# Zeros and scales of the down weights in one table row, two transfers a granule

## The chip, the cores and the metric

The kernel runs on one core of a Trainium2 chip. The metric is the device time of one execution in microseconds (us). Five engines work side by side, each through its own instruction queue: TensorE (PE, with its weight loads PEld), VectorE (DVE), ScalarE (ACT), GpSimd (POOL) and SyncE (SP). Here SP computes nothing; it issues nearly all DMA transfers.

## What is computed

The input x has 2048 rows of 1024 numbers. Both branches start from the layer norm of x, and their sum is added to x:

```python
xn = _layernorm(x)
out = x + s4_conv(xn) + ffn(xn)

def dequantize(W_q, scale, zero):      # W_q: two 4-bit numbers a byte
    w = stack([W_q >> 4 & 15, W_q & 15], -1)
    w = w.reshape(out, -1, 64)         # groups of 64
    return (w - zero[:, :, None]) * scale[:, :, None]

def ffn(x):                            # hidden 1024, inter 2752
    g = x @ dequantize(gate).T
    u = x @ dequantize(up).T
    return (silu(g) * u) @ dequantize(down).T
```

`s4_conv` is a long convolution whose kernel of 1024 taps is itself computed from a small state-space model, plus a multiple of xn. What matters here are the down weights: 1024 x 2752 numbers of 4 bits, with one zero and one scale for every 64 of them.

## The kernel before

**Precision.** PE works in fp16. Activations and weights are split into a high and a low fp16 part, and each product is made of three matmul passes (high·high, high·low, low·high). Matrix products are cut in blocks of two by two and formed with seven products in place of eight, so operands are also needed as sums and differences of blocks.

**Stages.** Until about 160 us x is loaded, normalised, and the first tiles are worked. From there to about 876 us runs the *gate/up stage*: `NJ = 21` tiles of the inner dimension (index j), each for two halves of the rows (index cp), so a step is called j_cp, such as 18_1. Beside it, in the same stage, the down weights are prepared and the convolution's kernel is computed in small DVE operations (tiles `s4p`, `s4n`). From 888 to 1004 us PE does the convolution (`cv`), from 1004 to 1325 us the down products.

**A gate/up step** (`gate_up`, seven products, each of twelve matmuls of 128x512) uses four PSUM banks, named A, B, C, D with the step's number. The scheme is a chain: ACT copies A to B, C to hb and B to D in turn; product 5 finishes D, then DVE adds D to hb (`hb_18_1<-D18_1,hb_18_1`); product 4 finishes C, ACT copies it to ha, DVE adds B (`ha<-B,ha`) and multiplies by silu of A (`ha<-ha,A`); product 3 refills D. A bank can be filled again only when DVE or ACT has read it, so PE waits for hb or ha when these are late. Products 5, 4 and 3 of one step are issued among the products of the next step.

**Gate and up weights** come in granules (tiles `w2` to `w42`): a granule is unpacked by DVE, multiplied by its scales on ACT in sixteen small instructions (`w<-w,sz`), summed on DVE, cast to a high part (ACT, `nat`), subtracted for the low part (DVE, `nat<-w,nat`), and transposed by DMA (`wf<-nat`).

**Down weights** are `2 * NPAIR = 20` granules, w43 to w62, worked in ten pairs (ga, gb) such as (w52, w62) by the generator `load_wd`. From j = `WD_FROM = 4` on, four of its steps are taken in each j_cp. For every granule:

- `load` fetches packed numbers (`raw`).
- `fetch_wd` allots the tile `w` ([128, 8, 256] fp32; two such buffers exist) and loads zeros into the part `w[:, 0:4]` and scales into `w[:, 4:8]`. Both come out of the table `SZT` in DRAM and are spread by DMA over 64 partitions each: partitions 0 to 63 take one half of the table's row (b = 0), 64 to 127 the other (b = 1). Then DVE unpacks nibbles (`qn`), and a DMA transposes them (`raw<-qn`).
- `dequant` makes `x4 = q - zeros` (`w<-raw,w`, the *subtract*), then `x4 * scales` (`w<-w` on 128x1024, the *multiply*).
- After that come sums and differences, casts on ACT (`nd<-w`), low parts on DVE (`nd<-w,nd`), and stores `WD<-nd`.

Of a pair, ga is fetched near the end of the pair before, gb at the pair's own start.

**The table** is made once by `scales_t`: zeros and scales of all twenty granules are loaded (`t0`), DVE writes them in another order to `t1` (scales times 1024), transposes 32x32 blocks, and four transfers store the table. Its shape is `SZT [2*NPAIR, 2, 2, 8, 128]`, with axes granule, w (scale or zero), b, c, h.

**Order.** Instructions are not issued in the order of the source. The kernel is built under a tile framework with `schedule_with_timeline_sim=True`: a planner with its own model of each instruction's duration chooses the order on each engine's queue when the program is built, within data dependencies and buffer counts. On the chip each queue runs strictly in that order: an instruction that waits holds up everything behind it on its engine. Nearly every instruction is recorded through the helper class `Engine` and so appears as line L77.

Of the kernel before, what the change touches and what calls it, by code (L numbers as in the profile page):

```python
# [41 lines left out]
G_WD = G_MIX + 1  # L42
# [45 lines left out]
def build(nc, tc, x, xp, raw_d, sz_d, par_d, vct_d, tab_d, csrow_d, out):  # L88
# [3 lines left out]
    with es:  # L92
# [11 lines left out]
        SZT = dr.tile([2 * NPAIR, 2, 2, 8, P], F32, name="SZT")  # L104
# [10 lines left out]
        SP, G, PE = Engine(tc, nc.sync), nc.gpsimd, Engine(tc, nc.tensor)  # L115
# [22 lines left out]
        def wtemp(kind, shape, dtype, name):  # L138
            return home[kind].tile(shape, dtype, tag=kind, name=name, **({"bufs": szbufs[0]} if kind == "sz" else {}))
# [148 lines left out]
        with ea:  # L288
# [47 lines left out]
            def sums(w, b_side):  # L336

                op = ALU.subtract if b_side else ALU.add
                V.tensor_tensor(w[:, 4], w[:, 0], w[:, 2], ALU.subtract)
                V.tensor_tensor(w[:, 2], w[:, 2], w[:, 3], op)  # L340
                if b_side:
                    V.tensor_tensor(w[:, 5], w[:, 0], w[:, 2], ALU.subtract)
                else:
                    V.tensor_tensor(w[:, 5], w[:, 2], w[:, 0], ALU.subtract)
                V.tensor_tensor(w[:, 6], w[:, 1], w[:, 5], ALU.subtract)
# [91 lines left out]
            def scales_t():  # L437

                n = 2 * NPAIR
                t0, t1 = (wtemp("nat", [P, n, 2, 16], F32, f"szt{i}") for i in range(2))  # L440
                SP.dma_start(t0, sz_d[G_WD : G_WD + n].rearrange("n p w c -> p n w c"))

                for i in range(2):
                    src, dst = t0[:, :, i].rearrange("p n (c b) -> p n c b", b=2), t1[:, :, i].rearrange("p n (b c) -> p n c b", b=2)
                    V.tensor_scalar(dst, src, (WS, 1.0)[i], None, ALU.mult)
                V.transpose(t0.rearrange("p n w c -> p (n w c)"), t1.rearrange("p n w c -> p (n w c)"))
                for a in range(4):
                    SP.dma_start(
                        SZT.rearrange("n w b c h -> (w b c) n h")[:, :, 32 * a : 32 * a + 32],
                        t0[32 * a : 32 * a + 32].rearrange("p n w c -> p n (w c)"),  # L450
                    )

            def lag(n=1):

                n += len(tails)
                while len(tails) < n:
                    yield
# [3 lines left out]
            def load_wd(u):  # L461


                pr, kq = divmod(u, 2)
                ga, gb = (G_WD + 2 * p + kq for p in (pr, pr + NPAIR // 2))
                tt, sub = V.tensor_tensor, ALU.subtract

                def load(gi):
                    raw = rawd[gi] = wtemp("raw", [P, 16, 32], I32, f"raw{gi}")
                    SP.dma_start(raw, raw_d[gi].rearrange("p (a b) -> p a b", a=16))  # L470

                def fetch_wd(gi):


                    raw = rawd.pop(gi)
                    w = wtemp("wd", [P, 8, 256], F32, f"w{gi}")
                    for i in range(2):
                        for b in range(2):
                            SP.dma_start(w[64 * b : 64 * b + 64, 4 * i : 4 * i + 4].rearrange("p f c -> p (f c)"),
                                         SZT[gi - G_WD, 1 - i, b].rearrange("c h -> (c h)").partition_broadcast(64))  # L480
                    q = wtemp("raw", [P, 16, 2, 32], I16, f"qn{gi}")
                    low = raw.bitcast(I16).rearrange("p a (b c) -> p a b c", c=2)[:, :, :, 0]
                    V.tensor_scalar(q[:, :, 0, :], low, 4, 15, ALU.logical_shift_right, ALU.bitwise_and)
                    V.tensor_scalar(q[:, :, 1, :], low, 15, None, ALU.bitwise_and)
                    qt = raw.bitcast(I16).rearrange("p a b -> p (a b)").rearrange("p (a b) -> p a b", a=8)
                    SP.dma_start_transpose(qt, q.rearrange("p a b c -> p (a b c)"))
                    return w, qt

                def dequant(w, qt):
                    x4 = w[:, 0:4]  # L490
                    tt(x4, qt.rearrange("p (f a) b -> p f (a b)", f=4), x4, sub)
                    tt(x4, x4, w[:, 4:8], ALU.mult)

                blocks = lambda w: w.rearrange("p f (m c) -> p f m c", m=2)
                nats = {}

                def hi(i, src):
                    nats[i] = wtemp("nat", [P, 7, 2, P], F16, f"nd{u}_{i}")
                    A.copy(nats[i][:, :, 0], src)

                def lo(i, src):
                    nat = nats.pop(i)
                    tt(nat[:, :, 1], src, nat[:, :, 0], sub)
                    SP.dma_start(
                        WD2[i - 1][:, :, pr, kq].rearrange("f p a c -> p f (a c)"), nat.rearrange("p f a c -> p f (a c)")
                    )

                nxt = [G_WD + 2 * ((u + 1) // 2 + o) + (u + 1) % 2 for o in (0, NPAIR // 2)] if u + 1 < NPAIR else None
                if u == 0:
                    load(ga)  # L510
                    load(gb)
                    yield from lag()
                    ready_wd[ga] = fetch_wd(ga)
                    yield
                ready_wd[gb] = fetch_wd(gb)
                yield from lag(2 if u == 0 else 1)
                ma = ready_wd.pop(ga)
                with tc.issue_after(tails[-1].ins):
                    dequant(*ma)
                wa = blocks(ma[0][:, 0:7])  # L520
                yield
                sums(ma[0], True)
                hi(1, wa[:, :, 0])
                yield
                if nxt:
                    load(nxt[0])
                lo(1, wa[:, :, 0])
                tt(wa[:, :, 0], wa[:, :, 1], wa[:, :, 0], sub)
                hi(5, wa[:, :, 0])
                yield  # L530
                lo(5, wa[:, :, 0])
                mb = ready_wd.pop(gb)
                dequant(*mb)
                wb = blocks(mb[0][:, 0:7])
                yield
                sums(mb[0], True)
                hi(3, wb[:, :, 1])
                tt(wa[:, :, 1], wb[:, :, 1], wa[:, :, 1], sub)
                yield
                if nxt:  # L540
                    load(nxt[1])
                lo(3, wb[:, :, 1])
                hi(7, wa[:, :, 1])
                tt(wb[:, :, 1], wb[:, :, 1], wa[:, :, 0], sub)
                yield

                lo(7, wa[:, :, 1])
                hi(6, wb[:, :, 1])
                if nxt:
                    ready_wd[nxt[0]] = fetch_wd(nxt[0])  # L550
                yield
                hi(2, wb[:, :, 0])
                lo(6, wb[:, :, 1])
                yield
                lo(2, wb[:, :, 0])
                tt(wb[:, :, 0], wb[:, :, 0], wb[:, :, 1], sub)
                hi(4, wb[:, :, 0])
                yield
                lo(4, wb[:, :, 0])
                yield  # L560
# [406 lines left out]
            t0 = combine(0)  # L967
# [12 lines left out]
            run(combine(1))  # L980
            finish_h(1, 1, h1b, h1c)
            scales_t()
            early.close()
            we.close()
# [105 lines left out]
        for b in range(2):  # L1090
            for n in range(2):
                p0 = 64 * b + 32 * n
                base = KP[:, 128 - 64 * b - 62 - n :]
                src = bass.AP(base.tensor, base.offset, [[2, 32], [base.ap[0][0], 2], [1, 1024]])
# [15 lines left out]
        for a0, b0 in ((128, 384), (640, 384)):  # L1110
            a, b = ([band[:, i, c : c + 384] for i in range(2)] for c in (a0, b0))
# [67 lines left out]
        for cp in range(2):  # L1179
# [7 lines left out]
            for c in range(2):  # L1187
                for k in range(2):
                    a, b = ([xc[2 * c][:, i, m, :] for i in range(2)] for m in (k, k + 2))
# [219 lines left out]
```

## Time and profile before

| | us |
|---|---|
| median of three runs | 1329.95 |
| lowest and highest | 1327.34, 1331.86 |
| the profiled execution | 1331.74 |
| its span (first to last instruction) | 1330.0 |
| PE busy | 1274.0 (96%) |
| DVE busy | 987.9 (74%) |
| ACT busy | 669.2 (50%) |
| POOL busy | 182.8 (14%) |

The mean clock granted to PE is 0.990 of full speed. The share of busy time is an average over stages; what a change inside the gate/up stage is worth is read from PE's holes in that stage.

Some durations of single instructions that the argument uses are, from the timeline:

| engine | instruction | us |
|---|---|---|
| PE | twelve matmuls of one product, 128x512 | 2.75 |
| ACT | sixteen scalings `w<-w,sz` | 5.41 |
| ACT | a cast of 128x896 | 0.94 |
| DVE | subtract or multiply of a granule, 128x1024 | 1.22 |
| DVE | one operation on hb or ha, 128x512 | 0.68 |
| DVE | a low part, 128x896 | 1.09 |
| SP | issue of one `w<-SZT` (median) | 0.607 |

A line of the timeline gives start, duration, engine, source line, operation, output and inputs by the program's names, shape, and a count where several of a kind follow each other. In brackets stands how long the engine sat idle before it, and what released it. `SPq` is SP's queue of DMA issues; the duration there is that of the issuing, not of the transfer. How long a transfer takes from issue to landing is in the page's list of DMA issues.

### The profile page before, as it was taken

What the parts mean: (1) busy time and instruction counts of PE and PEld (TensorE: products, weight loads), DVE (VectorE), ACT (ScalarE), POOL (GpSimd) and SP (SyncE); (2) the same over time, 40 slices, a digit from 0 to 9 for tenths busy, and PEclk for the clock granted to TensorE, in tenths of its full rate; (3) what the DMA queues carried; (4) which work ended last, traced back from release to release, by engine and by line L of the source; (5) the groups of instructions that cost most, each with busy time, mean ns of one, the idle gap of its engine ahead of it and who ended that gap; (6) DMA issues with size and microseconds to landing.
All of it is one profiled execution on the core that took longest, in us unless ns stands there. A gap on an engine that the chain in (4) does not pass through costs nothing. (4 is left out here: it accounts for less than half of the span.)

```text
span 1330.0 us, 20904 instructions
## 1 busy us (share of the span) xinstructions
PE 1274.0 (96%) x7880; PEld 751.9 (57%) x7880; DVE 987.9 (74%) x1344; ACT 669.2 (50%) x1208; POOL 182.8 (14%) x267
## 2 busy tenths in 40 slices
PE   5999899999999899989989998999999999999998
PEld 5644344444444344444444443456558888888887
DVE  6779967486886877786878777462738898779792
ACT  4867566656656474766568475420204433443330
POOL 3230001010100000000111000000000032256440
PEclk8999899999999999999999998999999999999999
DMA  6791958469887988888798887765837779799981
GB/s 225 173 218 31 196 152 186 97 163 251 212 229 159 240 217 207 223 210 232 191 264 224 216 215 180 216 213 187 333 122 292 273 202 265 238 262 274 285 181 48
DMA packets 358401, 276.04 MB, mean 208 GB/s; under 512 B 211668, under 2 KB 304668, under 8 KB 354204
## 3 DMA queue, kind: packets, MB, share of 16 engines
q1 hardware_dynamic: 335676, 261.59, 70.6%
q0 software_dynamic: 21760, 10.49, 6.6%
q10 hardware_dynamic: 864, 2.62, 0.5%
q8 instruction: 62, 1.02, 0.3%
q14 instruction: 39, 0.32, 0.1%
HBM read 132.36 MB, written 94.84 MB: 171 GB/s over the span
## 5 line engine op out<-in xcount | busy, mean ns | idle before, releaser
L77 PEld LDWEIGHTS <-wf 128*128 128x128 f16 x3960 | 375.7, 99 | 467.8 <-issue 45.2
L77 PEld LDWEIGHTS <-g 128*128 128x128 f16 x2940 | 287.6, 98 | 33.5 <-issue 0.2
L77 ACT ACTIVATE w<-w,sz 128x64 f32<-128x64 int32 x640 | 217.9, 427 | 74.9 <-DVE w L77 58.3
L77 PE MATMUL A<-x,wf 128*128 128x512 f16 x912 | 215.2, 385 | 13.4 <-ACT ha L77 5.3
L77 PE MATMUL D<-x,wf 128*128 128x512 f16 x912 | 211.5, 380 | 14.1 <-DVE hb L77 12.1
L77 PE MATMUL C<-x,wf 128*128 128x512 f16 x912 | 208.0, 381 | 2.8 <-DVE ha L77 2.6
L77 ACT CAST g<-a 128x2560 f16<-128x2560 f32 x42 | 97.5, 2324 | 182.1 <-PE cv L77 52.6
L77 PE MATMUL A<-b,g 128*128 128x256 f16 x1680 | 185.9, 273 | 0.0
L77 DVE TENSOR_TENSOR w<-w 128x256 f32<-128x256 f32 (+2 forms) x272 | 136.9, 527 | 61.2 <-ACT w L77 54.7
L77 DVE TENSOR_TENSOR g<-a,g 128x2560 f16<-128x2560 f32 x42 | 118.4, 2821 | 30.9 <-ACT g L77 30.9
L1261 POOL DMA_DIRECT2D out<-o x64 | 78.8, 2139 | 360.7 <-DVE o L77 348.2
L322 POOL TENSOR_SCALAR sz<-sz 128x16 f32<-128x16 f32 x42 | 18.6, 443 | 673.2 <-DMA sz<-in_sz 622.7
L77 PE MATMUL B<-x,wf 128*128 128x512 f16 x456 | 106.7, 384 | 1.8 <-ACT B L77 1.8
L77 ACT CAST nat<-w 128x896 f16<-128x896 f32 x76 | 68.3, 935 | 72.9 <-issue 34.4
L77 ACT CAST nd<-w 128x896 f16<-128x896 f32 x70 | 64.1, 933 | 68.9 <-DVE w L77 47.6
L77 DVE TENSOR_TENSOR nat<-w,nat 128x896 f16<-128x896 f32 x76 | 81.0, 1087 | 19.3 <-ACT nat L77 19.1
L77 PE MATMUL D<-b,g 128*128 128x256 f16 x840 | 94.0, 273 | 0.0
L77 DVE TENSOR_TENSOR nd<-w,nd 128x896 f16<-128x896 f32 x70 | 75.5, 1086 | 16.3 <-ACT nd L77 16.0
L77 PEld LDWEIGHTS <-x 128*128 128x128 f16 x576 | 52.4, 98 | 23.7 <-issue 2.7
L77 DVE SCALAR_TENSOR_TENSOR p<-cv,p 128x512 f32<-128x512 f32 x32 | 21.9, 688 | 50.3 <-PE cv L77 44.9
L77 PE MATMUL cv<-band,x 128*128 128x512 f16 (+3 forms) x384 | 57.1, 299 | 0.0
L77 PE MATMUL g<-x,wf 128*128 128x128 f16 (+1 forms) x336 | 48.8, 293 | 1.7 <-ACT wf L82 0.8
(145 smaller groups left out, 1203.8 us busy)
## 6 DMA issues: line engine op xcount, KB each, us to landing
a<-HF SPq DMA_DIRECT2D x28, 1280.0 KB, 8.1
WD<-nd SPq DMA_DIRECT2D x70, 448.0 KB, 4.4
b<-WD SPq DMA_DIRECT2D x49, 640.0 KB, 5.9
w<-SZT SPq DMA_DIRECT2D x80, 256.0 KB, 5.7
raw<-in_raw SPq DMA_DIRECT2D x65, 256.0 KB, 3.8
HF<-ha SPq DMA_DIRECT2D x54, 256.0 KB, 2.9
HF<-s SPq DMA_DIRECT2D x40, 256.0 KB, 3.0
HF<-hb SPq DMA_DIRECT2D x36, 256.0 KB, 3.6
```

What stands on the lines that cost most here:

```text
L77: return method(*args, **kw)
L322: G.tensor_scalar(sz[:, 0], sz[:, 0], WS, None, ALU.mult)
L1261: G.dma_start(dst, o[:, q], accum_op=ALU.add)
```

## The change

The axes of the table become granule, b, i, c, h, where i = 0 is the zeros and i = 1 the scales. For one granule and one b, zeros and scales now lie side by side in 8 KB, as they do in the tile `w`. `fetch_wd` loads a granule with two transfers (64 partitions times 8 KB, 512 KB each) instead of four (64 partitions times 4 KB, 256 KB each). `scales_t` writes `t1` in the matching order.

```diff
-    for i in range(2):
-        src, dst = t0[:, :, i].rearrange("p n (c b) -> p n c b", b=2), t1[:, :, i].rearrange("p n (b c) -> p n c b", b=2)
+    t2 = t1.rearrange("p n w c -> p n (w c)").rearrange("p n (b i c) -> p n i c b", b=2, i=2)
+    for i in range(2):
+        src, dst = t0[:, :, i].rearrange("p n (c b) -> p n c b", b=2), t2[:, :, 1 - i]
         V.tensor_scalar(dst, src, (WS, 1.0)[i], None, ALU.mult)
...
     for a in range(4):
         SP.dma_start(
-            SZT.rearrange("n w b c h -> (w b c) n h")[:, :, 32 * a : 32 * a + 32],
+            SZT.rearrange("n b i c h -> (b i c) n h")[:, :, 32 * a : 32 * a + 32],
             t0[32 * a : 32 * a + 32].rearrange("p n w c -> p n (w c)"),
         )
...
-    for i in range(2):
-        for b in range(2):
-            SP.dma_start(w[64 * b : 64 * b + 64, 4 * i : 4 * i + 4].rearrange("p f c -> p (f c)"),
-                         SZT[gi - G_WD, 1 - i, b].rearrange("c h -> (c h)").partition_broadcast(64))
+    for b in range(2):
+        SP.dma_start(w[64 * b : 64 * b + 64].rearrange("p f c -> p (f c)"),
+                     SZT[gi - G_WD, b].rearrange("i c h -> (i c h)").partition_broadcast(64))
```

## The prediction

> **What bounds the kernel now.** I read the busy tenths of the page first, then the windows by stage, then who waits for whom, then the timeline round the longest waits.
>
> ```profile
> PE   5999899999999899989989998999999999999998
> DVE  6779967486886877786878777462738898779792
> PEclk8999899999999999999999998999999999999999
> ```
>
> Each digit is 33 us. TensorE (PE) is full almost throughout, and after about 876 us nothing else matters: the down products there have a busy PE from end to end. The windows (start:end, length, busy us of PE, PEld, DVE, ACT, POOL, then clock, DMA share, GB/s) say the same:
>
> ```profile
> 400.00:500.00 100.00, 91.91 (x443) 42.12 (x442) 77.14 (x126) 63.08 (x136) 7.89 (x18) 1.00 0.82 205
> 600.00:700.00 100.00, 92.84 (x422) 41.09 (x421) 76.62 (x128) 62.04 (x133) 9.54 (x15) 0.98 0.90 230
> 760.00:830.00 70.00, 63.52 (x282) 28.10 (x281) 51.14 (x78) 46.86 (x104) 3.17 (x9) 0.95 0.81 206
> 1004.00:1325.00 321.00, 321.00 (x2940) 287.49 (x2939) 254.58 (x169) 117.77 (x63) 98.41 (x80) 1.00 0.84 238
> ```
>
> So only PE's holes between 160 and 876 us can be won, some 6 to 8% of a window. What makes them, and what the table has to do with them, is in the waits (total us, times, longest) and in the table's row (shortest/median/longest issue in ns):
>
> ```profile
> PE D L77 <- DVE hb L77: 12.1, 4, 5.5
> DVE w L77 <- DMA w<-SZT: 32.9, 10, 8.3
> L77 SPq DMA_DIRECT2D w<-SZT x80: 445/607/2390, 165.8 to 799.3; - x80
> w<-SZT SPq DMA_DIRECT2D x80, 256.0 KB, 5.7
> ```
>
> VectorE (DVE) idles 32.9 us for the table, but an idle DVE costs nothing unless PE needs what is queued behind. The timeline shows where it does (start, length, what, idle before and its releaser):
>
> ```profile
> 796.76 3.17 SPq L77 DMA_DIRECT2D w<-SZT  x4
> 803.71 1.23 DVE L77 TENSOR_TENSOR w<-raw,w 128x1024 f32<-128x1024 int16 x1 [8.28 <-DMA w<-SZT]
> 804.86 0.68 DVE L77 TENSOR_TENSOR hb<-D,hb 128x512 f32<-128x512 f32 x1
> 805.59 1.86 PE L77 MATMUL D<-x,wf 128*128 128x512 f16 x4 [5.46 <-DVE hb L77]
> ```
>
> Granule w62: four transfers issued from 796.76, its subtract waits 8.28 us for zeros, hb_18_1 stands behind that subtract, and PE waits 5.46 us for the PSUM bank that hb_18_1 frees. Two smaller cases have the same shape, w56 and w60:
>
> ```profile
> 453.37 2.75 PE L77 MATMUL D<-x,wf 128*128 128x512 f16 x12 [2.58 <-DVE hb L77]
> 690.01 2.32 PE L77 MATMUL D<-x,wf 128*128 128x512 f16 x10 [3.41 <-DVE hb L77]
> ```
>
> **The change, part by part.** *Building the table* (scales_t, once, near 160 us): the same two scalings, one transpose and four writes; only destination strides differ. Priced 0: the nearest rows, these instructions themselves, are 0.45 us each, so the bounds are ±0.5. PE is covered by j = 2 and 3 there.
>
> *Loading it* (20 granules). Bytes stay at 1 MB a granule. Removed are 40 issues on SP's queue at 0.607 us, 24 us in all, 1.2 us a granule. SP is not on the chain except where a transfer is late, so this shows only through landing times. In the trace a granule's issues are 0.5 to 1.3 us apart and its four landings about 1.1 us apart (w60: the last three at 685.0, 686.2, 687.2).
>
> Here the Trainium skill speaks on both sides ("DMA: Bandwidth & Descriptors"). Section "Rules for kernel authors" says to coalesce many small transfers; section "Anatomy of one DMA" gives each a fixed cost of about 2 us. Two fewer would then bring 4 us a granule. The row says no: four 256 KB transfers land 1.1 us apart, so that cost overlaps, and the engines are full in these bursts (DMA share 1.13 in 340 to 350 us). The same section says that a completion is reported only after the last byte, which speaks **against** the change. Today zeros land some 2.2 us ahead of the granule's last transfer, and the subtract starts on them. Afterwards it needs both whole transfers. By the coalescing rule the subtract starts 1.8 us earlier (4 less 2.2), by the rows 1.0 later (2.2 less the 1.2 of saved issues). I take the rows. Packets grow from 4 to 8 KB; no SZT row shows that, so it is bounded: nothing gained, or 1.3 us a granule (8 KB packets of other transfers took 351 ns on average where two 4 KB SZT packets take 2 × 255; 128 packets on 16 engines). I take 0, since the landings are spaced as the bytes are.
>
> So the multiply, which always needed everything, may start about 1.2 us earlier, and the subtract 1.0 later. Alone this is a small loss on DVE.
>
> *Order.* What decides is that instruction order is chosen by a planner when the program is built, and it knows the new waits. Comparing both programs engine by engine: same instructions apart from the 40 issues, but from j = 6 on (after about 328 us) many stand in another order on DVE, ACT and PE. I walk through the places where PE stalls or where the order changes what PE needs, adding durations of the rows (subtract and multiply 1.22, hb or ha operation 0.68, twelve matmuls 2.75, sixteen ACT scalings 5.41). Ends are in brackets.
>
> - **w54, 329 to 339 us.** hb_6_1 now precedes the waiting subtract; ha_6_1, behind it, comes 0.5 earlier. PE's 1.32 stall at 339.0 shrinks: −0.5 (−1.6 to +0.3).
> - **w56, 446 to 463 us.** Now a reciprocal (1.75) and an ha operation fill the wait and hb_9_1 directly follows the subtract, no longer a multiply and a qn unpack (1.98 together). The 2.58 stall becomes about 1.5; ha_9_1 (1.81 stall at 463.1) also comes earlier. −1.9 (−3 to −0.5).
> - **j = 12/13, w58, 545 to 580 us.** Against the change: ACT now does w27's sixteen scalings before the ha_11_1 copy, and w28's fifteen and two nd casts before the hb_12_1 copy, while PE moves ten C12_1 matmuls ahead of A13_0. A new stall of some 3.3 us near 555, of which the old 2.0 at 559.9 is part, and 0.3 at w58: +1.5 (0 to +4).
> - **619 us.** C14_0 covers with five matmuls instead of nine while PE waits for ha_13_1 (3.02 now): four at 0.22 = +0.9 (0 to +2).
> - **w60, 675 to 698 us.** The fetch moves up about 3 us, and D15_1 is moved behind twenty-four matmuls of j = 16, 5.2 us of cover for the 3.41 stall. Late next: ha_15_0, behind w60's subtract, multiply and unpack. −2.5 (−3.4 to 0).
> - **w61, 732 to 755 us.** On SP the fetch is moved behind a weight transpose, an HF and a WD store; the fourth transfer, issued 14 us after the first (746.47), vanishes. Both w61 operations now precede hb_17_0, which PE needs only at 749.6 though it was done at 740.7. 0 (cover 9 us).
> - **w62, 785 to 820 us.** hb_18_1 and w52's subtract precede w62's, so PE's bank is free near 801. Late next: ha_18_1, behind w62's subtract and about four sums and multiplies. The whole granule lands near 804.5, so ha_18_1 ends near 811.9, and A19_1 starts there, not at 816.09: −4.1 (−7 to 0).
>
> Clock: "TensorE: Matmul & The Clock Gate", section "Part 1", has the clock halve after an idle window of about 3.4 us. The rows are less orderly:
>
> ```profile
> 340.00:350.00 10.00, 10.00 (x41) 4.18 (x39) 9.62 (x16) 10.00 (x24) 0.75 (x1) 0.83 1.13 222
> 690.00:700.00 10.00, 9.99 (x47) 4.57 (x47) 9.97 (x19) 3.02 (x5) 2.61 (x3) 1.00 0.92 229
> 800.00:810.00 10.00, 4.54 (x12) 1.61 (x11) 6.29 (x9) 1.84 (x5) 1.58 (x4) 0.72 0.54 131
> ```
>
> The third figure from the right is the granted clock: 0.72 after the 5.46 stall, 0.83 after one of only 1.32, 1.00 after 3.41. By the rule the 3.1 us that I leave before A19_1 keeps full clock, and −4.1 stands; by the rows a shorter stall can halve it, for up to 3.4 us of lost work, and −0.7 is left. I take −4.1, since w62's loss today followed the longest stall.
>
> **Sum:** −0.5 − 1.9 + 1.5 + 0.9 − 2.5 + 0 − 4.1 = −6.6 us. The profiled execution took 1331.74 us (span 1330.0 and 1.7 around it), 1.8 above the median of the runs, 1329.95. 1331.7 − 6.6 = **1325 us**.
>
> **Rivals.**
> *Slower: the subtract waits for scales too.* Place: DVE's queue at w54, w56, w60, w62, the four waits with PE behind. Price: 1.0 to 2.2 us each, middle 1.6, 6.4 in all. It decides once both transfers land more than about 1 us after today's zeros and the ha or hb behind has no other cover. 1331.7 + 6.4 = 1338. For it: landings spaced by bytes, and the new ACT order at j = 12. Against it: in the new order hb_6_1 and hb_18_1 stand ahead of the wait.
> *No change.* The 5.46 and 3.41 stalls go but return whole at the next bank (ha_18_1, ha_15_0); −0.5 − 1.9 + 1.5 + 0.9 = 0: 1331.
> *More.* 8 KB packets land 1.3 us sooner: the stalls of 5.46, 3.41 and 2.58 go, with half-clock work worth 3.3 behind the first: −14.8, 1317. Against it: full DMA engines.
> *It does nothing of the kind* can be excluded: the diff's 40 transfers are gone from SP's order.
>
> **Numbers.** Forecast 0.42 (own range 1320 to 1329), slower rival 0.33, no change 0.11, more 0.14. A measurement of this kernel tells 0.3%, 4 us, from no change: faster is below 1326, slower above 1334. The forecast lies on that edge, so two thirds of it (0.28) count as faster: 0.28 + 0.14 = 0.42; same 0.14 + 0.11 = 0.25; slower 0.33. Range 1316 to 1340: the sum's ends, with the ±0.5 for the table, reach −15.5 and +6.3, and it takes in the middles of both outer rivals.
>
> **What would show it.** The w<-SZT row should read x40, 512 KB, with 5 to 7 us to landing; DVE's waits for it should be as long or longer in sum. The wait of PE for hb should fall from 12.1 to about 3 us, that for ha rise; the window 760 to 830 gain busy share and clock, 500 to 600 lose some. I am wrong if the stalls for ha at j = 12 to 15 or 18 exceed the hb stalls that go, or if the order brings stalls at places I passed over.

## The result, and the profile after

| kernel | median us | lowest to highest | runs |
|---|---|---|---|
| before | 1330.04 | 1327.34 to 1332.57 | 6 |
| changed | 1344.68 | 1339.77 to 1346.87 | 6 |

The ratio is 1.010, with a 95% interval of 1.0086 to 1.0115: the change makes the kernel slower, by 14.6 us between the medians. The forecast was 1325, the range 1316 to 1340. The profiled execution of the changed kernel is the fastest of its six (1339.77, span 1338.0), so its trace shows 8.0 of these 14.6 us.

First PE's waits for ha and for the copies to B and D, before (total us, times, longest):

```profile
PE A L77 <- ACT ha L77: 5.3, 3, 3.0
...
PE A L77 <- DVE ha L77: 3.7, 3, 1.9
...
PE D L77 <- ACT D L77: 2.0, 1, 2.0
PE B L77 <- ACT B L77: 1.8, 3, 0.7
```

The same in the changed kernel, with the wait for hb:

```profile
PE A L77 <- ACT ha L77: 10.7, 6, 3.3
...
PE A L77 <- DVE ha L77: 8.2, 4, 3.9
PE B L77 <- ACT B L77: 7.6, 5, 3.2
...
PE D L77 <- ACT D L77: 5.2, 1, 5.2
...
PE D L77 <- DVE hb L77: 1.3, 3, 0.5
```

The wait for hb, 12.1 us before, is down to 1.3, as the new order promised. But each of the other four waits has grown: with hb, these five were 24.9 us before and are 33.0 now. The stalls went from one bank to the others and grew on the way.

The table's row (shortest, median and longest issue in ns), then its entry in the list of DMA issues (KB each, median us from issue to landing), then DVE's wait for it:

```profile
L77 SPq DMA_DIRECT2D w<-SZT x40: 461/903/1627, 165.1 to 808.9; - x40
```

```profile
w<-SZT SPq DMA_DIRECT2D x40, 512.0 KB, 7.3
```

```profile
DVE w L77 <- DMA w<-SZT: 33.1, 8, 8.5
```

Half as many issues, and the median issue takes 903 ns instead of 607. The medians don't give the saving, because some issues before took up to 2.39 us. Added up over the traces, the eighty issues took 62.2 us of SP's time and the forty take 38.1: the 24 us of the forecast, 1.2 a granule, were indeed saved. But DVE's wait is as long as before, and a transfer lands 7.3 us after its issue, not 5.7.

The place that looked best in the forecast, w62, in the changed kernel's timeline:

```profile
807.98 1.75 SPq L77 DMA_DIRECT2D w<-SZT  x2
...
817.24 1.23 DVE L77 TENSOR_TENSOR w<-raw,w 128x1024 f32<-128x1024 int16 x1 [6.88 <-DMA w<-SZT]
...
823.45 1.78 ACT L77 CAST nat<-w 128x896 f16<-128x896 f32 x2 [10.75 <-issue]
...
825.13 0.58 ACT L77 COPY D<-B 128x512 f32<-128x512 f32 x1
825.76 4.85 PE L77 MATMUL D<-x,wf 128*128 128x512 f16 x11 [5.21 <-ACT D L77]
```

From the first issue to the subtract are 9.26 us, where it was 6.95 before. Behind the subtract on DVE stand, among others, the sums of a gate/up granule; ACT idles 10.75 us before it casts them. The profile names no releaser for that wait, but the casts start 0.08 us after a group of these sums ends, here and in the trace of four transfers in the same order further down. Behind the casts stands the copy that frees bank D, and PE waits 5.21 us for that. DVE's queue has handed its lateness to ACT, and ACT to PE. The eleven matmuls then take 4.85 us, where twelve take 2.75 at full clock. The last of these windows of the changed kernel (clock third from the right) shows it. The other two answer the forecast's signs: 500 to 600 lost busy time and clock, as it said (93.80 us and 1.00 before), while 760 to 830 gained a little clock but lost busy time (63.52 us and 0.95 before), where it was to gain both:

```profile
500.00:600.00 100.00, 92.34 (x423) 41.39 (x422) 80.72 (x159) 57.84 (x127) 5.99 (x15) 0.97 0.88 210
760.00:830.00 70.00, 62.50 (x279) 27.57 (x278) 52.61 (x86) 40.07 (x85) 4.15 (x10) 0.96 0.83 200
820.00:830.00 10.00, 4.79 (x14) 1.65 (x13) 10.00 (x19) 4.67 (x8) 1.12 (x2) 0.69 0.61 119
```

### The profile page after: what moved, and what is told of

Same layout as the page of the kernel before. It is cut to its first block, busy times and chain, and to the rows that moved or that the text cites. A ratio compares the mean times of both kernels' runs of the same rounds, so it can differ in the third digit from the quotient of the medians.

```text
span 1338.0 us, 20845 instructions
## 1 busy us (share of the span) xinstructions
PE 1276.1 (95%) x7880; PEld 751.5 (56%) x7880; DVE 988.2 (74%) x1344; ACT 669.4 (50%) x1208; POOL 183.1 (14%) x267
## 5 line engine op out<-in xcount | busy, mean ns | idle before, releaser
L322 POOL TENSOR_SCALAR sz<-sz 128x16 f32<-128x16 f32 x42 | 23.7, 565 | 685.1 <-DMA sz<-in_sz 659.3
L77 DVE TENSOR_TENSOR nd<-w,nd 128x896 f16<-128x896 f32 x70 | 75.7, 1086 | 14.8 <-ACT nd L77 14.6
L77 DVE TENSOR_TENSOR w<-raw,w 128x1024 f32<-128x1024 int16 x20 | 24.4, 1220 | 46.0 <-DMA w<-SZT 33.1
```

Source lines behind the costliest of these rows:

```text
L77: return method(*args, **kw)
L322: G.tensor_scalar(sz[:, 0], sz[:, 0], WS, None, ALU.mult)
```

## The experiments

The change does two things at once: it makes the subtract wait for more, and it makes the planner choose another order. Both can be held apart. The order of a finished program was read out, engine by engine, and given to another source by chaining each instruction behind its predecessor (issue order only, no wait):

```diff
         build(nc, tc, *args, out)
+        pin_order(nc, tc)
...
+            for a, b in zip(seq, seq[1:]):
+                tc.add_manual_dep(b, a.name, info, reason="pin_order")
```

With it every instruction but the table's own loads stands where it stood in the program that lent the order; the loads of a granule take the place of the lender's. Where the lender's trace is kept, the traces bear this out: engine by engine they list the same operations and tiles in the same order.

**Transfers and order apart.** Two whole transfers in the old order:

> The change's two transfers of 512 KB and its table, with every other instruction on every engine held in the order of the kernel before. Theory A, the subtract now waits for whole transfers: the loss is here too, 1340 to 1346 us. Theory B, the planner's new order makes the loss and the transfers themselves nothing or a small gain: 1326 to 1332 us.

Measured: 1352.69 us, ratio 1.0162 (1.0146 to 1.0179). Four transfers in the changed kernel's order:

> The kernel before's four transfers of 256 KB and its table, with every other instruction held in the order of the changed kernel. Theory A: the loss goes, 1328 to 1334 us. Theory B: the loss stays, 1340 to 1348 us, since the order is that of the changed kernel and four issues take SP 1.2 us more a granule.

Measured: 1324.07 us, ratio 0.9949 (0.9936 to 0.9961). Both times lie outside the spans of theory A, but it has the cause right: the loss is the loads', and is larger than the result shows, +21 us in the old order. Of theory B only this holds, that the order matters: by itself it is a gain of some 7 us, which hides a part of the loss.

With the two transfers in the old order, w62 looks like this in the timeline; it is the very chain of the kernel before, only longer:

```profile
815.44 1.87 SPq L77 DMA_DIRECT2D w<-SZT  x2
...
825.25 1.23 DVE L77 TENSOR_TENSOR w<-raw,w 128x1024 f32<-128x1024 int16 x1 [12.38 <-DMA w<-SZT]
...
826.40 0.68 DVE L77 TENSOR_TENSOR hb<-D,hb 128x512 f32<-128x512 f32 x1
...
827.13 1.86 PE L77 MATMUL D<-x,wf 128*128 128x512 f16 x4 [8.59 <-DVE hb L77]
```

PE waits 8.59 us where it waited 5.46. Since the order is the same, the two traces can be compared granule by granule (us after the granule's first issue, for the granules of which both traces hold all four times):

| granule | subtract starts, before | subtract starts, two whole | last landing, before | last landing, two whole |
|---|---|---|---|---|
| w54 | 7.8 | 9.8 | 10.0 | 9.7 |
| w55 | 7.2 | 9.6 | 9.4 | 9.5 |
| w57 | 6.1 | 9.5 | 8.3 | 9.4 |
| w58 | 7.4 | 10.3 | 9.3 | 10.2 |
| w59 | 6.2 | 8.8 | 8.7 | 8.7 |
| w60 | 6.9 | 8.6 | 9.0 | 8.5 |
| mean | 6.9 | 9.4 | 9.1 | 9.3 |

The whole granule is not there sooner, and the subtract starts 2.5 us later. The reason is in the DMA engines, which are busy all the while, with four transfers as with two: here are the windows of w62's loads in the kernel before and in this one (DMA share second from the right):

```profile
797.00:806.00 9.00, 3.54 (x17) 1.45 (x16) 2.29 (x4) 4.84 (x14) 0.73 (x3) 0.91 0.97 270
```

```profile
816.00:825.00 9.00, 2.54 (x12) 1.07 (x11) 0.00 (x0) 3.27 (x9) 0.73 (x3) 0.76 1.00 244
```

Nor do larger packets help: the table's packets of 8 KB took 559 ns on average in this trace, where two of 4 KB took 2 x 255 before.

PE's stall at w54 grew from 1.32 to 3.78 us, at w56 from 2.58 to 5.46, at w57 from 0.26 to 3.09, at w58 from 1.88 to 4.30, at w59 from 0.74 to 2.83, at w60 from 3.41 to 4.30, at w62 from 5.46 to 8.59: seven granules, 16.7 us together, of which smaller stalls elsewhere give some back. All kernels run the same 7880 matmuls, so a longer busy time of PE points to a slower clock, and the granted clock agrees:

| profiled execution | span | PE busy | PE idle | mean granted clock |
|---|---|---|---|---|
| before | 1330.0 | 1274.0 | 56.0 | 0.990 |
| two whole, old order | 1349.0 | 1280.8 | 68.2 | 0.982 |
| changed kernel | 1338.0 | 1276.1 | 61.9 | 0.989 |
| four, new order | 1321.7 | 1273.2 | 48.5 | 0.991 |

Of the 19.0 us between the first two, 12.2 are idle time and 6.8 are lost clock. The window round the longest stall in the second kernel has little over half of full speed:

```profile
820.00:830.00 10.00, 2.87 (x7) 0.99 (x7) 4.75 (x7) 0.00 (x0) 1.38 (x3) 0.53 0.46 88
```

**Is it the waiting or the size?** Four transfers as before, in the old order, but scales ahead of zeros: the subtract needs the last one, yet nothing is larger and no issue is saved.

```diff
-                    for i in range(2):
+                    for i in (1, 0):
                         for b in range(2):
                             SP.dma_start(w[64 * b : 64 * b + 64, 4 * i : 4 * i + 4]...
```

> The kernel before, its four transfers and its order, but scales issued ahead of zeros, so that the subtract needs the last transfer of a granule. Theory A: 2.2 us later at each wait that PE feels, the same loss as with whole transfers or more, 1338 to 1346 us. Theory B: within 3 us of the kernel before.

Measured: 1355.31 us, ratio 1.0184 (1.017 to 1.0198), as slow as two whole transfers, and above theory A's span. Then half by half, so that the subtract needs the third transfer of four (`for b` outside, `for i` inside):

> The kernel before, its table, its four transfers and its order, but issued half by half (zeros and scales of the first half, then of the second), so that the subtract needs the third of four transfers. Theory A': every us that the subtract starts later costs in proportion; the second transfer needed gave 1331, the fourth 1355, so the third gives about 1343 us, 1338 to 1348. If only the very last transfer mattered (the last receipt, or the multiply behind it), it would stay at 1331 to 1335 us.

Measured: 1344.22 us, ratio 1.0116 (1.0099 to 1.0133), halfway. Second, third or fourth transfer needed: 1331, 1344, 1355 us. In the traces the subtract of the eight granules w54 to w60 and w62 starts 7.0, 8.4 and 9.1 us after the first issue on average (9.6 with two whole transfers). So it is not a last receipt alone that costs, but the delay as it grows. And the new table alone, made and stored as in the change, loaded with four transfers:

> The change's table (zeros and scales side by side), made and stored as the change does it, but loaded with four transfers of 256 KB, zeros first, in the order of the kernel before. Theory A: the layout is nothing, 1329 to 1333 us. Rival: reading 4 KB out of 8 KB rows or the other writing costs something by itself, above 1335 us.

Measured: 1330.8 us, ratio 1.0005 (0.9995 to 1.0016). The layout is nothing, and neither is the pinning itself.

**Two transfers cut the other way.** Zeros for all 128 partitions, then scales, old order:

```diff
+                    for i in range(2):
+                        SP.dma_start(w[:, 4 * i : 4 * i + 4]...,
+                                     SZT[gi - G_WD, 1 - i].rearrange("b c h -> b (c h)").unsqueeze(1).to_broadcast([2, 64, 1024]))
```

> Two transfers of 512 KB cut the other way: zeros for all 128 partitions, then scales for all 128, packets of 4 KB, in the order of the kernel before. The subtract waits for the first alone. Theory A: as the kernel before or up to 4 us faster, 1326 to 1331 us, against 1340 or more with the change's own two in this order. Theory B: 1326 to 1331 us as well, and no more than 2 us from the change's own two in this order.

Measured: 1629.72 us, ratio 1.224. This is far outside every span and says nothing on either theory, since such a transfer runs far below the others' rate. Stretches in which little else moves, in this kernel's windows (DMA share of 16 engines and GB/s last):

```profile
471.00:474.00 3.00, 3.00 (x16) 1.37 (x14) 0.00 (x0) 0.00 (x0) 0.00 (x0) 1.00 0.13 52
...
489.00:492.00 3.00, 3.00 (x11) 1.20 (x10) 1.21 (x2) 0.00 (x0) 0.00 (x0) 0.73 0.13 48
```

A share of 0.13 is what two busy engines of sixteen make. The source's slowest dimension here is b, of size 2. The Trainium skill ("DMA: Bandwidth & Descriptors", section "Rules for kernel authors") says that an outermost dimension smaller than 16 confines a transfer to that many engines; the share agrees. A cut of this kind that uses all engines wasn't tried, so it stays open whether two large transfers with the zeros first would gain anything.

**Was the new order luck?** Three more orders were lent to the kernel before with its four transfers, zeros first; each is the planner's for a source in which the subtract waits for something else.

> The kernel before with its four transfers, zeros first, in the order that the planner makes when scales are issued ahead of zeros, so that it takes the subtract to wait for the last of four transfers. If orders planned for a late subtract are better in general, 1320 to 1328 us, as with the changed kernel's order (1324); if that order was luck, anywhere within 8 us of the kernel before's 1331.

Measured: 1320.38 us, ratio 0.9938 (0.992 to 0.9957).

> The same with the order that the planner makes for transfers issued half by half, where it takes the subtract to wait for the third of four. Late planning helps: 1322 to 1330 us. Luck: within 8 us of 1331 on either side.

Measured: 1325.31 us, ratio 0.996 (0.995 to 0.9971).

> The same with the order that the planner makes for two transfers cut by part, zeros first, where it takes the subtract to wait for the first of two. Late planning helps: no gain here, 1328 to 1335 us, since the plan is not a late one. Luck: within 8 us of 1331 on either side.

Measured: 1329.73 us, ratio 0.9999 (0.9987 to 1.0011). All three came out as "late planning helps" had it, and with the changed kernel's own order that makes three orders planned for a late subtract, all of them gains, and one planned for an early one, which is none. But this doesn't settle it. The second and third results lie within the span given for luck as well; only 1320.38 lies outside. And the three late orders are near relatives: by the tile names in the traces, 75 and 79 of the 7880 matmuls stand elsewhere in the other two than in the changed kernel's order, while 215 to 242 stand elsewhere in the three than in the kernel before. They are not three separate draws. That late planning helps is likely, not shown.

**Does size add anything?** Scales first in the planner's own order for it:

> Scales issued ahead of zeros in four transfers, in the order that the planner makes for it. If the change's loss is the later subtract less what the planner makes good, this one loses as much as the change, 1340 to 1350 us, against 1355 in the order of the kernel before. If the size of the transfers matters, it stays below 1337 us.

Measured: 1333.52 us, ratio 1.0034 (1.0021 to 1.0047). A miss: the planner makes good nearly all of it, while for two whole transfers it made good a third. Either large transfers cost something of their own, or this order is the better one. So each loading was run in the other's order:

> The change's two transfers and table in the order that the planner makes for scales-first (1320 with zeros first, 1333.5 with scales first). If the change only had the less lucky order of the two, this one gives about 1333, 1330 to 1337 us. If two large transfers cost more than a late subtract by themselves, it stays near the changed kernel, 1340 to 1348 us.

Measured: 1334.54 us, ratio 1.0031 (1.0022 to 1.004).

> Four transfers, scales ahead of zeros, in the changed kernel's order (1324 with zeros first, 1344.7 with two whole transfers). If only the lateness of the subtract and the order count, as much as the changed kernel, 1341 to 1348 us; if the two large transfers add a cost of their own, 1330 to 1338 us.

Measured: 1340.27 us, ratio 1.007 (1.0058 to 1.0082), just under the first span and clear of the second. All medians together:

| order planned for | four, zeros first | two whole | four, scales first |
|---|---|---|---|
| zeros first (before) | 1330.0 | 1352.7 | 1355.3 |
| two whole (the change) | 1324.1 | 1344.7 | 1340.3 |
| scales first | 1320.4 | 1334.5 | 1333.5 |

Along a row, the second and third columns differ by −2.6, +4.4 and +1.0 us: size and number of transfers have no steady effect (the +4.4 is not explained), while waiting for the last transfer costs 13 to 25 us in every row. Down a column the order decides. The best of all is the last row's first column: the kernel before, with the order planned for scales first, faster than before by 0.6% and than the change by 1.8%.

In the changed kernel's order with four transfers, w62 is the same chain as in the changed kernel, but shorter:

```profile
795.21 3.07 SPq L77 DMA_DIRECT2D w<-SZT  x4
...
802.60 1.22 DVE L77 TENSOR_TENSOR w<-raw,w 128x1024 f32<-128x1024 int16 x1 [4.39 <-DMA w<-SZT]
...
808.78 1.78 ACT L77 CAST nat<-w 128x896 f16<-128x896 f32 x2 [8.24 <-issue]
...
811.10 2.75 PE L77 MATMUL D<-x,wf 128*128 128x512 f16 x12 [2.69 <-ACT D L77]
```

The subtract starts 7.39 us after the first issue instead of 9.26, PE stalls for 2.69 instead of 5.21, and twelve matmuls behind it take 2.75 us: the clock holds.

## Why the prediction was wrong

*What bounds the kernel.* Right. All that changed lies in PE's holes of the gate/up stage, and DVE's wait for the table is where it starts.

*Building the table at 0.* Right: 1.0005 for the layout alone.

*Loading it: this step failed.* It said that the subtract starts "1.0 later (2.2 less the 1.2 of saved issues)", called that "a small loss on DVE", and gave it no term of its own in the sum. The 2.2 was right. The 1.2 of issues was saved too, but on SP's queue alone: it did not reach the landings. In the same order, the whole granule landed 9.3 us after the first issue against 9.1, so nothing came off the 2.2; the subtract started 2.5 us later, and that cost 21 us. The landings 1.1 us apart were read correctly against the coalescing rule, but the same row says that bytes, and not issues, set the pace. What spoke against the change, completion only after the last byte, was what decided.

Two details of that step. In the Trainium skill ("DMA: Bandwidth & Descriptors", section "Anatomy of one DMA") the 2 us of fixed cost are given for transfers that GpSimd issues; the table's loads are issued by SP, so the figure did not apply as it stood, and no run here shows such a cost. And the window of 340 to 350 us, cited for full DMA engines, holds none of the table's loads; the window of w62's loads, with a share of 0.97, shows what it was cited for.

*The w62 line of the walk carries the same error.* It let the whole granule land near 804.5, which is 7.7 us after the first issue; in the changed kernel the subtract, which waits for it, starts at 9.3. In place of the −4.1 came a new stall of 5.21 with half clock behind it.

*Only four places.* The slower rival had the right mechanism and place (DVE's queue behind the subtract), but counted w54, w56, w60 and w62 and 1.6 us for each, 6.4 in all. In the old order seven granules reached PE, most with 2 to 3 us, and 6.8 us of lost clock came on top: 21 us. A wait that PE doesn't feel today (w57: 5.87 us of idle DVE, 0.26 of PE) is slack that is nearly used up, not a wait that costs nothing when it grows.

*The order.* The sum of the walk, −6.6 us, is what the order gives when the subtract is early: 0.9949 is −6.8 us (−8.5 to −5.2). It was in effect made for four transfers in the new order, not for the change. That the two agree is luck, for the terms don't. Here are PE's stalls of over 0.4 us at each place, added up:

| place | forecast | before | four, new order | changed kernel |
|---|---|---|---|---|
| w54 | −0.5 | 1.32 | none | 3.37 |
| w56 | −1.9 | 4.39 | none | 1.55 |
| j = 12/13, w58 | +1.5 | 5.46 | 2.63 | 7.22 |
| 619 us | +0.9 | 3.02 | 3.85 | 1.39 |
| w60 | −2.5 | 3.41 | 2.33 | 3.29 |
| w62 | −4.1 | 5.46 | 2.69 | 5.21 |
| A8_1, 378 us | not foreseen | none | 3.71 | 1.59 |
| w59, 640 to 660 us | not foreseen | 0.74 | 2.13 | 3.91 |
| B17_0, 725 us | not foreseen | none | 2.76 | 2.76 |

With early data w54, w56 and j = 12/13 went better than forecast, w60 and w62 worse, and new stalls took the difference. Late next at w62 was ACT's copy to D behind the casts, not ha_18_1. The last column is the forecast's own sign of being wrong: stalls at places that it had passed over.

*Clock.* It was left out, with −4.1 standing at full clock. In the changed kernel the eleven matmuls behind the 5.21 stall took 4.85 us; over its whole trace PE is busy 2.1 us longer than before. It costs more where more stalls grow, 6.8 us with two whole transfers in the old order.

## What to carry to other kernels

Merging transfers that feed different instructions makes the first of these wait for all the bytes; where the landings of separate transfers are spaced as their bytes are, as they were here, there is little fixed cost to win back, and time saved on the issuing queue need not reach the landings. Ask of each merged transfer which consumer needed only its front, by how much it is later, and what stands behind that consumer on its queue, also where no one feels it today. Where a planner chooses the order, measure a change's loads and its order apart by pinning one: here a gain of 7 us and a loss of 21 lay under a loss of some 14, and an order planned for late data, run with early data, gave the best kernel.

## What the runs showed of the hardware

Two transfers of 512 KB and four of 256 KB, in the same order of instructions and with the DMA engines busy (shares 1.00 and 0.97), land a granule at about the same time, 9.3 and 9.1 us after the first issue. The median issue of the larger one occupies SP for longer (903 and 778 ns in the two traces, against 607), though the shortest are alike (461, 470 and 445). A transfer of the same 512 KB whose source has a slowest dimension of 2 moved at about 50 GB/s, with a DMA share of 0.13.

The length of a stall alone does not tell whether the clock drops after it. Before the change, the window behind a stall of 1.32 us has a clock of 0.83; with four transfers in the new order, the ten us behind a stall of 3.71 have full clock:

```profile
380.00:390.00 10.00, 10.00 (x49) 4.52 (x47) 8.95 (x13) 8.74 (x21) 0.54 (x2) 1.00 1.13 243
```

The 0.83 is one stretch of 3.41 us at half clock in the kernel before:

```profile
340.11:343.52 3.41, 3.41 (x10) 1.21 (x9) 3.33 (x7) 3.41 (x6) 0.64 (x1) 0.50 1.11 218
```
